# A two-layer graph network: layer 1's weighted rows in buffers of their own, layer 0's gathers by spans

## The chip, the cores and the metric

The kernel runs on one core of one Trainium2 chip. The metric is the device time of one execution in microseconds (us). The core has five engines that run side by side, each through its own list of instructions: TensorE (PE, matrix products), VectorE (DVE, elementwise work), ScalarE (ACT, functions such as exp), GpSimd (POOL, which here mainly issues indirect transfers, the gathers) and SyncE (SP, which issues the other transfers). They wait for each other through semaphores: an instruction that others depend on counts a semaphore up when it is done, and the waiting engine stands still until the count is reached.

## The reference

Everything is float32. x has N = 6250 nodes with C = 256 features; there are E = 100000 edges (src, dst, weight), sorted by dst. Cut to what matters:

```python
# layer 0
xn = layernorm(x)
agg = segment_sum(edge_weight[:, None] * xn[src], dst, N)     # edge loop of layer 0
x = x + relu(agg @ W + b) + linear_attention(xn)
x = x + ffn_top1_of_32(layernorm(x))
# layer 1
xn = layernorm(x)
h = (xn @ W1).reshape(N, 4, 64)                               # 4 heads
e = leaky_relu(h_l[src] + h_r[dst])                           # per edge and head
m = segment_max(e, src, N)
ex = exp(e - m[src])
att = ex / (segment_sum(ex, src, N)[src] + 1e-16)
out = segment_sum(att[:, :, None] * h[dst], src, N)           # edge loop of layer 1
x = x + out + key_value_mix(xn)
x = x + ffn_top2_of_16(x)
```

In layer 1 the edges are grouped by src, the row that is added to; the gathered row is h[dst]. The division by the sum of ex comes after the sums.

## The kernel before, in words

The nodes are 49 tiles of 128 rows. The edges, sorted on the chip by the row that they are added to, are 782 tiles of 128 edges (one edge per partition). Both edge loops do for a tile of edges: gather 128 rows of a table in memory by an indirect transfer on POOL (`gather`, L293 to 296; in the trace its line is L294), make a one-hot matrix S [128 edges x 128 rows] on VectorE, and multiply S^T by the gathered rows on PE into a PSUM tile `ps`; VectorE adds `ps` to the accumulator in SBUF. A float32 product of one tile is two PE instructions in the profile.

**Layer 0's edge loop** (L782 to 800) goes over 196 spans of four tiles. For each tile it gathers into `xg` (24 buffers of one tile), makes S from position and weight in one VectorE instruction (L791, 16 buffers), and multiplies (L793) into the span's `ps` (3 buffers); then two accumulates (L796). Beside it runs the linear attention, one step every second span, and one step of the sort for layer 1 every third span. A gather into a buffer of `xg` waits until the product that read the buffer 24 tiles ago is done, so each product signals.

**Layer 1's edge loop** (L1107 to 1427) goes over 25 chunks of GT = 32 tiles (24 full ones and one of 14). CR = C + 4 = 260 columns: 256 features and four more, which hold h_r of the row until they are replaced by ex, so that one product adds up both the weighted rows and the sums of ex. Three functions are called per chunk, `fetch` one chunk ahead:

- `fetch` (L1236) gathers the chunk's rows of `h_d`, 8 tiles per buffer, into 4 of 8 buffers `hgs`, and loads `pen`, `fr` and the broadcast positions `lob`. Six of the buffers lie in `xs`, a tile [128, 49, 256] that is otherwise the node array; two lie in `hg2`. Then, per 8 tiles: `hw` (L1269, L1271), a transposed one-hot `ST` (L1278) and 8 small products `pe` (L1281), which spread h_l of the rows to the edges.
- `weigh` (L1285) adds the scores (`z`, L1294), finds the segment maxima by scans and transposes on VectorE, and takes exp on ScalarE twice (L1360): once into a PSUM tile `exi`, once into the last four columns of the gathered rows. `fc` (L1363) corrects the accumulator at a chunk's border.
- `gain` (L1377) takes each of the chunk's four groups of 8 tiles: multiplies the gathered rows in place by exp (L1385), makes S (L1388, 2 buffers), does 8 products into `ps` (L1393, 3 buffers) and two accumulates (L1397). After each group it advances a generator, `keys_values` (L1134), which is layer 1's mix: products L1169, L1194, L1228, `sq` L1172, `sd` L1178 and so on.

A gather into a buffer thus waits for the product on PE that read the tile two chunks before. Tile's scheduler puts the instructions of each engine in order and places the semaphores; PE, VectorE and ScalarE each count one semaphore.

After the loop an If (L1680; a fallback, `general_attention`, that these inputs do not take) and then `expert_pairs`, the second feed-forward. It first loads the node array back from memory into `xs` by seven transfers on SP's queue (L1692, L1693; 0.9 MB each, the last smaller), then the weights `w2` (16 loads of 512 KB), the router's weights (L91), and goes on with `finals` (L1726, L1728), the router (product L1714 and its transposes) and the experts.

Of the kernel before, what the change touches and what calls it, by code (L numbers as in the profile page):

```python
# [8 lines left out]
F32 = mybir.dt.float32  # L9
I32 = mybir.dt.int32  # L10
U32 = mybir.dt.uint32
AF = mybir.ActivationFunctionType
OP = mybir.AluOpType
# [7 lines left out]
P = 128  # L21
N = 6250
C = 256
E = 100000
NT = 49
LAST = N - (NT - 1) * P
CH = 7
# [9 lines left out]
TS = (E + P - 1) // P  # L37
SC = 1024
LB = 13
GT = 32  # L40
# [12 lines left out]
def gps_kernel(ctx, tc, x, src, dst, edge_weight, g0_W, g0_b, m0_WqT, m0_WkvT, m0_WpT, m0_bp,  # L53
# [3 lines left out]
    nc = tc.nc  # L57
    cst = ctx.enter_context(tc.tile_pool(name="cst", bufs=1))


    iota = cst.tile([P, P], F32, name="iota")
# [11 lines left out]
    eps = cst.tile([P, 1], F32, name="eps")  # L73
    nc.vector.memset(eps, LN_EPS)

    xs = cst.tile([P, NT, C], F32, name="xs")
    nc.vector.memset(xs[:, NT - 1, :], 0.0)

    CR = C + 4
# [213 lines left out]
    def gather(o, tab, idx):  # L293
        nc.gpsimd.indirect_dma_start(  # L294
            out=o, out_offset=None, in_=tab,
            in_offset=bass.IndirectOffsetOnAxis(ap=idx, axis=0))
# [284 lines left out]
    xw_d = tc.dram_tile([N, C], F32, name="xw_d")  # L581
# [37 lines left out]
    with tc.tile_pool(name="l0", bufs=1) as lp:  # L619
        lo0 = lp.tile([P, 4 * QA], F32, name="lo0")  # L620
        wt0 = lp.tile([P, 4 * QA], F32, name="wt0")
        idx0 = lp.tile([P, 4 * QA], I32, name="idx0")
# [84 lines left out]
        with tc.tile_pool(name="g0w", bufs=4) as gw, tc.tile_pool(name="e0", bufs=1) as ep, \  # L707
# [74 lines left out]
            for b in range(QA):  # L782
                if b % 8 == 0:
                    off = group_values(own0, b, DVE, (NT - 1) * C)
                ps = gps.tile([P, C], F32, name="ps")
                tiles = range(4 * b, min(4 * b + 4, TS))
                for t in tiles:
                    xg = gw.tile([P, C], F32, name="xg", bufs=24)
                    gather(xg, xw_d, idx0[:, t:t + 1])
                    S = gw.tile([P, P], F32, name="S", bufs=16)  # L790
                    nc.vector.tensor_scalar(S, iota, lo0[:, t:t + 1], wt0[:, t:t + 1],  # L791
                                            op0=OP.is_equal, op1=OP.mult)
                    nc.tensor.matmul(ps, S, xg, start=t == tiles[0], stop=t == tiles[-1])  # L793
                for a, m in ((agg, in0[0]), (agg[:, C:], in0[1])):
                    a = a[:, ds(off[b % 8], C)]
                    nc.vector.scalar_tensor_tensor(a, ps, m[:, b:b + 1], a, op0=OP.mult, op1=OP.add)  # L796
                if b % 2 == 1:
                    next(beside, None)
                if b % 3 == 1:
                    next(order, None)  # L800
# [301 lines left out]
            *slots_f0, layer1_rows, order1)  # L1102


    xsf = xs.rearrange("p t c -> p (t c)")
    HU = 8 * CR
    with tc.tile_pool(name="g1", bufs=1) as gp, tc.tile_pool(name="g1b", bufs=2) as gw:  # L1107
        idx1 = gp.tile([P, 8 * QB], I32, name="idx1")
        lo1 = gp.tile([P, 8 * QB], F32, name="lo1")
        hl = gp.tile([P, NT + 1, 4], F32, name="hl")  # L1110
        hg2 = gp.tile([P, 2 * HU], F32, name="hg2")
        nc.sync.dma_start(idx1, idx_d)
        nc.sync.dma_start(lo1, lo_d)
        nc.sync.dma_start(hl, hl_d.rearrange("(t p) k -> p t k", p=P))
        hlf = hl.rearrange("p t k -> p (t k)")

        hgs = [(xsf[:, i * HU:(i + 1) * HU] if i < 6 else hg2[:, (i - 6) * HU:(i - 5) * HU])
               .rearrange("p (i c) -> p i c", c=CR) for i in range(8)]
        zc = gp.tile([P, 1], F32, name="zc")
        nc.vector.memset(zc, 0.0)  # L1120
        nc.scalar.copy(acc, zc.to_broadcast([P, (NT + 1) * CR]))
        with tc.tile_pool(name="g1bp", bufs=1, space=PSUM) as pps:
# [113 lines left out]
            def fetch(t0, n):  # L1236

                hg = []
                for u in range(0, n, 8):
                    h8 = hgs[(t0 + u) // 8 % 8]  # L1240
                    for i in range(min(8, n - u)):
                        t = t0 + u + i
                        gather(h8[:, i, :], h_d, idx1[:, t:t + 1])
                    hg.append(h8)


                pen = gw.tile([P, 33], F32, name="pen")
                fr = gw.tile([4, 2, GT * B], F32, name="fr")
                if n < GT:
                    nc.vector.memset(pen, LOW)  # L1250
                for b in range(B):
                    nc.sync.dma_start(pen[32 * b:32 * b + n, :], bass.AP(
                        tensor=pen_d.tensor, offset=pen_d.offset + t0 * P + 32 * b,
                        ap=[[P, n], [1, 33]]))
                nc.sync.dma_start(fr[:, :, :n * B], bass.AP(
                    tensor=fr_d.tensor, offset=fr_d.offset + t0 * B,
                    ap=[[0, 4], [TS * B, 2], [1, n * B]]))
                brk = gw.tile([P, 2, 4, 32], F32, name="brk")
                for d in range(2):
                    nc.vector.tensor_copy(brk[:, d], pen[:, None, d:d + 32].to_broadcast([P, 4, 32]))  # L1260
                    nc.vector.memset(brk[:, d, :, 31 * d:31 * d + 1], LOW)
                pe = pes[:, t0 // GT % 2]
                ofs = group_values(own1[1], t0 // 8, DVE, (NT - 1) * 4, (n + 7) // 8)
                for u in range(0, n, 8):
                    m = min(8, n - u)
                    q = (t0 + u) // 8

                    hw = gw.tile([P, 4], F32, name="hw", bufs=4)
                    nc.vector.tensor_scalar(hw, hlf[:, ds(ofs[u // 8], 4)], in1[0][:, q:q + 1], None,  # L1269
                                            op0=OP.mult)  # L1270
                    nc.vector.scalar_tensor_tensor(hw, hlf[:, 4:][:, ds(ofs[u // 8], 4)],  # L1271
                                                   in1[1][:, q:q + 1], hw, op0=OP.mult, op1=OP.add)
                    lob = gw.tile([P, 8 * P], F32, name="lob")
                    nc.sync.dma_start(lob[:, :m * P], bass.AP(
                        tensor=lob_d.tensor, offset=lob_d.offset + (t0 + u) * P,
                        ap=[[0, P], [1, m * P]]))
                    ST = gw.tile([P, 8 * P], F32, name="ST")
                    nc.vector.tensor_scalar(ST[:, :m * P], lob[:, :m * P], pcol, None,  # L1278
                                            op0=OP.is_equal)
                    for i in range(m):  # L1280
                        nc.tensor.matmul(pe[:, :, u + i], ST[:, i * P:(i + 1) * P], hw,  # L1281
                                         start=True, stop=True)
                return hg, pe, pen, fr, brk

            def weigh(t0, n, hg, pe, pen, fr, brk, before_):  # L1285
# [70 lines left out]
                nc.vector.tensor_tensor(z[:, :, :n], z[:, :, :n], mx[:, :, :n], op=OP.subtract)  # L1356
                for u in range(0, n, 8):
                    m = min(8, n - u)
                    for o in (exs[t0 // GT % 2][:, u:u + m, :], hg[u // 8][:, :m, C:]):
                        nc.scalar.activation(o, z[:, :, u:u + m].rearrange("p k t -> p t k"), AF.Exp)  # L1360
                if before_ is not None:
                    fc = gw.tile([P, 4], F32, name="fc")
                    nc.scalar.activation(fc, tr[:, 2, :4], AF.Exp)  # L1363
# [13 lines left out]
            def gain(t0, n, hg):  # L1377

                ex = exs[t0 // GT % 2]
                off = group_values(own1[0], t0 // 8, DVE, (NT - 1) * CR, (n + 7) // 8)  # L1380
                for u in range(0, n, 8):
                    m = min(8, n - u)
                    h8 = hg[u // 8]
                    v = h8[:, :m, :C].rearrange("p i (k d) -> p i k d", k=4)
                    nc.vector.tensor_tensor(v, v, ex[:, u:u + m, :, None].to_broadcast([P, m, 4, 64]),  # L1385
                                            op=OP.mult)
                    S = gw.tile([P, 8, P], F32, name="S")
                    nc.vector.tensor_tensor(  # L1388
                        S[:, :m, :], iop[:, None, :].to_broadcast([P, m, P]),
                        lo1[:, t0 + u:t0 + u + m, None].to_broadcast([P, m, P]), op=OP.is_equal)  # L1390
                    ps = pps.tile([P, CR], F32, name="ps", bufs=3)
                    for i in range(m):
                        nc.tensor.matmul(ps, S[:, i, :], h8[:, i, :], start=i == 0, stop=i == m - 1)  # L1393
                    q = (t0 + u) // 8
                    for a, k in ((acc, in1[0]), (acc[:, CR:], in1[1])):
                        a = a[:, ds(off[u // 8], CR)]
                        nc.vector.scalar_tensor_tensor(a, ps, k[:, q:q + 1], a,  # L1397
                                                       op0=OP.mult, op1=OP.add)
                    beside.step()
# [280 lines left out]
    with tc.If(bads1[0] > 0):  # L1680
        general_attention()


    def expert_pairs(ne, nk, hid, w1_d, b1_d, w2_d, b2_d, rw_d, rb_d, ns, xs_d, ys_d):
        lead, step = 104, 3
# [3 lines left out]
        xn_t = xn_d.rearrange("(t p) c -> p t c", p=P)  # L1689
        with ExitStack() as ctx1:  # L1690
            fp = ctx1.enter_context(tc.tile_pool(name="f1", bufs=1))
            for t0 in range(0, NT, CH):  # L1692
                nc.sync.dma_start(xs[:, t0:t0 + CH, :], xs2_d[:, t0:t0 + CH, :])  # L1693
            wt = fp.tile([P, 2, NT], F32, name="wt")
            pi = fp.tile([P, nk * NT], I32, name="pi")
            oi = [fp.tile([1, ns], I32, name=f"own{n}") for n in (1, wn, nf, C)]
# [162 lines left out]
```

## Time and profile before

| | |
|---|---|
| median of 3 runs | 4324.72 us (4312.03 to 4339.27) |
| the profiled execution | 4330.09 us, its span 4328.3 us |
| PE busy | 2628.5 us (61%) |
| VectorE busy | 2106.9 us (49%) |
| POOL busy | 1827.0 us (42%) |
| ScalarE busy | 488.9 us (11%) |
| layer 0's edge loop, first to last gather | 124 to 1282 us |
| layer 1's edge loop, first to last gather | 1872 to 3409 us; its last instruction about 3460 us |
| stage 130 to 1300 us | PE 767, VectorE 564, ScalarE 75, POOL 749 us busy |
| stage 1870 to 3460 us | PE 869, VectorE 767, ScalarE 104, POOL 746 us busy |

How to read it: an engine's busy time is what it worked, not what it waited; the idle time before an instruction is put down to what ended it, its releaser. "remote" means that the instruction waited for a semaphore and that the trace has no instruction whose end fits the moment at which the count came; "issue" means that it waited for nothing that the profile shows. A line such as `L294 POOL DMA_INDIRECT xg<-xw_d,idx x782 | 754.0, 964 | 527.7 <-issue 161.8` reads: line 294, on POOL, 782 gathers from xw_d into xg, busy 754.0 us in all, 964 ns each; POOL was idle 527.7 us ahead of them, most of it (161.8) ended by nothing visible.

### The profile page before, as it was taken

How to read it: one execution, taken by the hardware profiler on the slowest of the kernel's cores; microseconds unless marked ns; L12 is line 12 of the kernel's file. 1: busy time of each engine (PE TensorE's matmuls, PEld its weight loads, DVE VectorE, ACT ScalarE, POOL GpSimd, SP SyncE). 2: the span in 40 equal slices, each digit the busy share in tenths (PEclk: the TensorE clock that was granted, in tenths of full speed). 3: DMA queues.
4: the chain of work that ended last, by engine and by line, in shares of the span. 5: the costliest groups of instructions: out<-in, count | busy, mean ns of one | idle time of the engine just before them, and what ended most of it. 6: DMA issues, size and time to landing. Idle time of an engine off the chain costs nothing. (4 is left out here: it accounts for less than half of the span.)

```text
span 4328.3 us, 43935 instructions
## 1 busy us (share of the span) xinstructions
PE 2628.5 (61%) x11725; PEld 2151.6 (50%) x11725; DVE 2106.9 (49%) x6129; ACT 488.9 (11%) x1386; POOL 1827.0 (42%) x1864
## 2 busy tenths in 40 slices
PE   5466566776776596736465456447556434999920
PEld 4344344555555354625454455446445433788820
DVE  5345454454446566714454455445444654222247
ACT  3000000000001121300111010100000011222200
POOL 0566666666652202253534544454454226000046
PEclk9778787778775565855666666666566655999965
DMA  6633333333321444743333333334444353555544
GB/s 206 203 113 105 103 106 100 98 94 98 101 84 34 155 141 124 204 126 117 110 101 113 109 108 112 109 107 143 144 128 137 92 176 134 189 187 189 185 146 127
DMA packets 355794, 557.64 MB, mean 129 GB/s; under 512 B 91419, under 2 KB 244664, under 8 KB 355270
## 3 DMA queue, kind: packets, MB, share of 16 engines
q0 software_dynamic: 89760, 245.19, 20.3%
q1 hardware_dynamic: 229342, 272.12, 19.7%
q10 hardware_dynamic: 36424, 37.28, 2.6%
q8 instruction: 104, 1.70, 0.2%
q14 instruction: 164, 1.34, 0.1%
HBM read 438.88 MB, written 115.49 MB: 128 GB/s over the span
## 5 line engine op out<-in xcount | busy, mean ns | idle before, releaser
L294 POOL DMA_INDIRECT xg<-xw_d,idx x782 | 754.0, 964 | 527.7 <-issue 161.8
L294 POOL DMA_INDIRECT xs<-h_d,idx x590 | 562.7, 954 | 756.0 <-PE ps L1393 520.4
L1281 PE MATMUL pe<-hw,ST 128*128 128x4 f32 x1564 | 329.0, 341 | 445.7 <-issue 103.4
L1281 PEld LDWEIGHTS pe<-hw,ST 128*128 128x128 f32 x1564 | 329.6, 318 | 455.7 <-issue 102.2
L294 POOL DMA_INDIRECT yg<-f_ys,pi x147 | 172.9, 1176 | 815.5 <-SPq L1792 484.6
L793 PE MATMUL ps<-xg,S 128*128 128x256 f32 x1564 | 456.4, 438 | 72.0 <-DVE S L791 33.4
L793 PEld LDWEIGHTS ps<-xg,S 128*128 128x128 f32 x1564 | 329.8, 223 | 156.9 <-issue 66.0
L1397 DVE SCALAR_TENSOR_TENSOR acc<-ps,in,acc 128x260 f32 x196 | 94.6, 483 | 575.4 <-remote 481.7
L1393 PE MATMUL ps<-xs,S 128*128 128x260 f32 x1180 | 311.5, 431 | 50.9 <-issue 41.8
L796 DVE SCALAR_TENSOR_TENSOR acc<-ps,in,acc 128x256 f32 x392 | 187.3, 478 | 280.8 <-remote 140.5
L1393 PEld LDWEIGHTS ps<-xs,S 128*128 128x128 f32 x1180 | 255.2, 219 | 100.6 <-issue 42.7
L791 DVE TENSOR_SCALAR S<-iota,lo,wt 128x128 f32<-128x128 f32 x782 | 251.2, 352 | 101.7 <-PE ps L793 50.1
L392 POOL DMA_INDIRECT f_xs<-xn,d_pi x147 | 153.1, 1041 | 280.8 <-ACT xT L127 109.9
L294 POOL DMA_INDIRECT hg<-h_d,idx x192 | 183.8, 957 | 97.3 <-remote 49.7
L1781 PE MATMUL y<-w,h 128*128 x856 | 215.4, 392 | 12.6 <-ACT h L1774 9.6
L1769 PEld LDWEIGHTS hT<-xTt,w 128*128 128x128 f32 x1712 | 212.3, 195 | 6.1 <-ACT xTt L127 0.5
L1769 PE MATMUL hT<-xTt,w 128*128 128x128 f32 x1712 | 213.1, 278 | 0.2 <-ACT xTt L127 0.2
L1777 DVE TENSOR_SCALAR h<-hT,b1T 128x128 f32<-128x128 f32 x214 | 74.8, 350 | 254.6 <-ACT h L1774 253.7
L1781 PEld LDWEIGHTS y<-w,h 128*128 128x128 f32 x856 | 149.1, 189 | 48.3 <-ACT h L1774 23.5
L1385 DVE TENSOR_TENSOR xs<-xs,exi 128x2048 f32<-128x2048 f32 x74 | 168.0, 2270 | 6.7 <-ACT exi L1360 6.5
L743 PE MATMUL ctx<-v,k 128*128 128x129 f32 (+1 forms) x196 | 45.1, 368 | 171.1 <-ACT v L741 110.9
L125 PE MATMUL tr<-ident,xt 128*128 128x128 f32 x350 | 86.5, 338 | 80.7 <-DMA xt<-f_xs 80.1
(346 smaller groups left out, 4280.7 us busy)
## 6 DMA issues: line engine op xcount, KB each, us to landing
w<-in_L_ffn_w SPq DMA_DIRECT2D x123, 512.0 KB
lob<-lob_d SPq DMA_DIRECT2D x97, 512.0 KB
xT<-xnT SPq DMA_DIRECT2D x196, 128.0 KB
xt<-f_xs SPq DMA_DIRECT2D x107, 128.0 KB
f_ys<-y SPq DMA_DIRECT2D x107, 128.0 KB
xnT<-xT SPq DMA_DIRECT2D x98, 128.0 KB
xg<-xw_d,idx POOLq DMA_INDIRECT x782
xs<-h_d,idx POOLq DMA_INDIRECT x590
```

The source lines that it names most:

```text
L125: nc.tensor.transpose(p[:, c, :], t[:, c * P:(c + 1) * P], ident)
L294: nc.gpsimd.indirect_dma_start(out=o, out_offset=None, in_=tab, in_offset=bass.IndirectOffsetOnAxis(ap=idx, axis=0))
L392: st = nc.gpsimd.indirect_dma_start(out=xs_d, in_=xn[:r, i, :], in_offset=None, out_offset=bass.IndirectOffsetOnAxis(ap=pi[:r, t, k:k + 1] ...
L791: nc.vector.tensor_scalar(S, iota, lo0[:, t:t + 1], wt0[:, t:t + 1], op0=OP.is_equal, op1=OP.mult)
L793: nc.tensor.matmul(ps, S, xg, start=t == tiles[0], stop=t == tiles[-1])
L796: nc.vector.scalar_tensor_tensor(a, ps, m[:, b:b + 1], a, op0=OP.mult, op1=OP.add)
L1281: nc.tensor.matmul(pe[:, :, u + i], ST[:, i * P:(i + 1) * P], hw, start=True, stop=True)
L1385: nc.vector.tensor_tensor(v, v, ex[:, u:u + m, :, None].to_broadcast([P, m, 4, 64]), op=OP.mult)
L1393: nc.tensor.matmul(ps, S[:, i, :], h8[:, i, :], start=i == 0, stop=i == m - 1)
L1397: nc.vector.scalar_tensor_tensor(a, ps, k[:, q:q + 1], a, op0=OP.mult, op1=OP.add)
L1769: nc.tensor.matmul(hT[:, f, :], w1[:, c, f * P:(f + 1) * P], xT[:, c, :], start=c == 0, stop=c == 1)
L1781: nc.tensor.matmul(yp, h[:, f, :], w2e[:, f * C:(f + 1) * C], start=f == 0, stop=f == nf - 1)
```

## The change

There are three parts.

1. The gathers of layer 1 go into buffers `h8` of their own (8 buffers of 8 tiles). The multiply by exp no longer works in place but writes to `w8` (2 buffers), and the products read `w8`. The second set of exps goes; a copy on ScalarE puts ex into the last columns of `w8` in its place.
2. `xs` now belongs to a pool of its own, which is closed ahead of layer 1's loop and opened again after the If. The seven loads into it stand there.
3. In layer 0 a span of four tiles shares one buffer of `xg` (6 buffers) and of S (4 buffers). The gathers and one-hots of a span are issued from the last tile to the first, and its four products follow together.

The buffer counts make the look-ahead of the gathers 64 tiles in layer 1, as before, and 6 spans of 4 tiles in layer 0, where there were 24 tiles.

```diff
-    xs = cst.tile([P, NT, C], F32, name="xs")
+    def stream():
+        pool = ExitStack()
+        return pool, pool.enter_context(tc.tile_pool(name="xp", bufs=1)).tile(
+            [P, NT, C], F32, name="xs")
+    xpool, xs = stream()
...
-                tiles = range(4 * b, min(4 * b + 4, TS))
-                for t in tiles:
-                    xg = gw.tile([P, C], F32, name="xg", bufs=24)
-                    gather(xg, xw_d, idx0[:, t:t + 1])
-                    S = gw.tile([P, P], F32, name="S", bufs=16)
-                    nc.vector.tensor_scalar(S, iota, lo0[:, t:t + 1], wt0[:, t:t + 1],
+                n = min(4, TS - 4 * b)
+                xg = gw.tile([P, 4, C], F32, name="xg", bufs=6)
+                S = gw.tile([P, 4, P], F32, name="S")
+                for i in reversed(range(n)):
+                    t = 4 * b + i
+                    gather(xg[:, i, :], xw_d, idx0[:, t:t + 1])
+                    nc.vector.tensor_scalar(S[:, i, :], iota, lo0[:, t:t + 1], wt0[:, t:t + 1],
                                             op0=OP.is_equal, op1=OP.mult)
-                    nc.tensor.matmul(ps, S, xg, start=t == tiles[0], stop=t == tiles[-1])
+                for i in range(n):
+                    nc.tensor.matmul(ps, S[:, i, :], xg[:, i, :], start=i == 0, stop=i == n - 1)
...
+    xpool.close()
...
-                    h8 = hgs[(t0 + u) // 8 % 8]
+                    h8 = gw.tile([P, 8, CR], F32, name="h8", bufs=8)
...
-                    for o in (exs[t0 // GT % 2][:, u:u + m, :], hg[u // 8][:, :m, C:]):
-                        nc.scalar.activation(o, z[:, :, u:u + m].rearrange("p k t -> p t k"), AF.Exp)
+                    nc.scalar.activation(exs[t0 // GT % 2][:, u:u + m, :],
+                                         z[:, :, u:u + m].rearrange("p k t -> p t k"), AF.Exp)
...
-                    h8 = hg[u // 8]
-                    v = h8[:, :m, :C].rearrange("p i (k d) -> p i k d", k=4)
-                    nc.vector.tensor_tensor(v, v, ex[:, u:u + m, :, None].to_broadcast([P, m, 4, 64]),
-                                            op=OP.mult)
+                    w8 = gw.tile([P, 8, CR], F32, name="w8", bufs=2)
+                    nc.vector.tensor_tensor(
+                        w8[:, :m, :C].rearrange("p i (k d) -> p i k d", k=4),
+                        hg[u // 8][:, :m, :C].rearrange("p i (k d) -> p i k d", k=4),
+                        ex[:, u:u + m, :, None].to_broadcast([P, m, 4, 64]), op=OP.mult)
+                    nc.scalar.copy(w8[:, :m, C:], ex[:, u:u + m, :])
...
-                        nc.tensor.matmul(ps, S[:, i, :], h8[:, i, :], start=i == 0, stop=i == m - 1)
+                        nc.tensor.matmul(ps, S[:, i, :], w8[:, i, :], start=i == 0, stop=i == m - 1)
...
+    xpool, xs = stream()
+    ctx.enter_context(xpool)
+    for t0 in range(0, NT, CH):
+        nc.sync.dma_start(xs[:, t0:t0 + CH, :], xs2_d[:, t0:t0 + CH, :])
...
-            for t0 in range(0, NT, CH):
-                nc.sync.dma_start(xs[:, t0:t0 + CH, :], xs2_d[:, t0:t0 + CH, :])
```

More of the change, by code (lines that the diff above doesn't have):

```diff
@@ L1102, in gps_kernel @@
             *slots_f0, layer1_rows, order1)
-    xsf = xs.rearrange("p t c -> p (t c)")
-    HU = 8 * CR
+    xpool.close()
     with tc.tile_pool(name="g1", bufs=1) as gp, tc.tile_pool(name="g1b", bufs=2) as gw:
@@ L1110, in gps_kernel @@
         hl = gp.tile([P, NT + 1, 4], F32, name="hl")
-        hg2 = gp.tile([P, 2 * HU], F32, name="hg2")
         nc.sync.dma_start(idx1, idx_d)
@@ L1115, in gps_kernel @@
         hlf = hl.rearrange("p t k -> p (t k)")
-        hgs = [(xsf[:, i * HU:(i + 1) * HU] if i < 6 else hg2[:, (i - 6) * HU:(i - 5) * HU])
-               .rearrange("p (i c) -> p i c", c=CR) for i in range(8)]
         zc = gp.tile([P, 1], F32, name="zc")
```

## The prediction

> **What bounds the kernel now.** I read the page's busy shares first: TensorE (PE) 61%, VectorE (DVE) 49%, GpSimd (POOL) 42%. No engine is full, so some wait decides, and the groups tell which.
>
> ```profile
> L294 POOL DMA_INDIRECT xg<-xw_d,idx x782 | 754.0, 964 | 527.7 <-issue 161.8
> L294 POOL DMA_INDIRECT xs<-h_d,idx x590 | 562.7, 954 | 756.0 <-PE ps L1393 520.4
> L1397 DVE SCALAR_TENSOR_TENSOR acc<-ps,in,acc 128x260 f32 x196 | 94.6, 483 | 575.4 <-remote 481.7
> L1393 PE MATMUL ps<-xs,S 128*128 128x260 f32 x1180 | 311.5, 431 | 50.9 <-issue 41.8
> ```
>
> In layer 1's loop POOL waits 520 us for PE's products and VectorE's accumulate 482 us for something "remote". The tile's view gives first and last gather: layer 0 from 124 to 1282 us, layer 1 from 1872 to 3409 us. The timeline of VectorE in one chunk shows the stall (start, length, engine, line; in brackets the idle time before and its releaser); of the accumulates it has the first of each of the four groups:
>
> ```profile
> 2305.62 2.28 DVE L1385 TENSOR_TENSOR xs<-xs,exi 128x2048 f32<-128x2048 f32 x1
> ...
> 2316.56 0.49 DVE L1397 SCALAR_TENSOR_TENSOR acc<-ps,in,acc 128x260 f32 x1 [2.00 <-PE ps L1393]
> ...
> 2321.44 0.49 DVE L1397 SCALAR_TENSOR_TENSOR acc<-ps,in,acc 128x260 f32 x1 [0.67 <-PE ps L1393]
> ...
> 2341.80 0.49 DVE L1397 SCALAR_TENSOR_TENSOR acc<-ps,in,acc 128x260 f32 x1 [17.98 <-remote]
> ...
> 2351.11 0.49 DVE L1397 SCALAR_TENSOR_TENSOR acc<-ps,in,acc 128x260 f32 x1 [6.12 <-remote]
> ...
> 2356.81 0.21 DVE L1294 TENSOR_TENSOR z<-xs,pe 128x32 f32<-128x32 f32 x1 [5.21 <-remote]
> ...
> 2377.24 2.27 DVE L1385 TENSOR_TENSOR xs<-xs,exi 128x2048 f32<-128x2048 f32 x1
> ```
>
> And PE and POOL in the same stretch:
>
> ```profile
> 2310.10 9.93 PE L1393 MATMUL ps<-xs,S 128*128 128x260 f32 x32
> 2319.87 7.18 PE L1393 MATMUL ps<-hg,S 128*128 128x260 f32 x32
> 2343.82 3.57 PE L1281 MATMUL pe<-hw,ST 128*128 128x4 f32 x16 [16.78 <-DVE hw L1269]
> ```
> ```profile
> 2311.59 0.94 POOL L294 DMA_INDIRECT xs<-h_d,idx  x1 [8.90 <-PE ps L1393]
> 2312.83 0.95 POOL L294 DMA_INDIRECT xs<-h_d,idx  x1 [0.30 <-issue]
> ...
> 2353.82 0.95 POOL L294 DMA_INDIRECT hg<-h_d,idx  x1 [0.30 <-issue]
> ```
>
> PE is through with all 32 products at 2327.05 (2319.87 + 7.18), yet the last accumulate starts at 2351.11: the products were done and their signal was not there. That is 24 us of "remote". The reader sees why beside it: the gathers run without a gap from 2311.59, one per 1.25 us (0.95 + 0.30). In the first 9 us of such a run the products' signals come at once (the first group's ends at 2316.52, its accumulate starts at 2316.56), then some 2 to 4 us pass between one signal and the next. VectorE's own signals are not late. In layer 1 the third and fourth groups of a chunk are 10 to 27 us late throughout; in layer 0 the wait of L796 on "remote" is 140 us.
>
> From this chunk's first multiply (L1385) to the next are 71.6 us; over the loop the mean is 60.1 (2006.2 to 3447.8, 24 chunks). Of it PE is busy some 33 us, VectorE some 30, and 32 gathers at 1.25 are 40.
>
> **The change, part by part.** The profiled execution is 4330.1 us (span 4328.3), 5.4 above the median of 4324.7. I sum against it and take the 5 off.
>
> *Layer 1, products.* Now each of the 32 tiles' products of a chunk signals, since each gather into its rows waits for it. After: 4 signals, one per 8 tiles, and gathers wait for the multiply on VectorE alone. Worked by hand from the start t=0 of a chunk's first multiply, with the durations above: the multiply ends at 2.3 and releases 8 gathers, so the run of 32 starts there (before, at 6.0) and lasts 40 us at best. Group 1's products end at about 11 as now, signal at age 9 or less, on time. The third multiply now needs one of two w8 buffers, that is group 1's products; before, only its one-hot (L1388) did. It moves from 6.7 to some 11.5, group 3's products from 17.9 to 20 or so, group 4's from 21.4 to 25. Each added microsecond counts up to there: some +3 us. Then the signals: four instead of 32, at ages 9 to 23, by 2 to 4 us each as in the runs of now: the last accumulate starts at about 28, against 45.5 in the chunk shown. After it come 20 us (2356.81 to 2377.24: scores, scans, exps, the one-hots ST) as before: period 48. If the last signal takes 16 us, as one did in a free run (next paragraph), it starts at 36 and the period is 56. I take 52, the middle: neither row is nearer, the first has the same matmuls, the second the same gathers. That is 8.1 us off 60.1, over 23 chunks 186 us. The bounds: below, POOL alone; 668 of the 782 starts follow the last by under 1.3 us, so 782 x 1.25 = 978 against 1537 is 559 off, less 50 for the first chunk's two fetches and its weighing (they're in both): -510. Above: +127 (rival D).
>
> The row that speaks against me is at the start of this same loop. There the gathers wait for nothing and PE signals once per 8 tiles, which is what the change makes of the rest (VectorE, then PE):
>
> ```profile
> 1889.65 0.23 DVE L1269 TENSOR_SCALAR hw<-hl,in 128x4 f32 x1 [4.66 <-remote]
> 1906.48 0.23 DVE L1269 TENSOR_SCALAR hw<-hl,in 128x4 f32 x1 [15.89 <-remote]
> 1950.58 0.45 DVE L1269 TENSOR_SCALAR hw<-hl,in 128x4 f32 x1 [42.71 <-remote]
> ```
> ```profile
> 1883.42 6.99 PE L1281 MATMUL pe<-hw,ST 128*128 128x4 f32 x32 [1.13 <-DVE ST L1278]
> 1907.77 3.57 PE L1281 MATMUL pe<-hw,ST 128*128 128x4 f32 x16 [17.36 <-issue]
> ```
>
> Gathers ran from 1871.82 to about 1951. The matmuls that these wait for ended at 1887.0, 1890.4 and 1911.3: late by 2.6, 16 and 39 us, at ages 15, 19 and 39. So fewer signals do not suffice; what counts is how long gathers run unbroken, and the change takes away the pauses that PE's own waits put between them.
>
> *The exps.* Four exps into hg's columns go (0.256 us each), four copies into w8 come, which wait for group u-2's products. ScalarE is 104 us busy of 1590 in this loop; a copy by the nearest row (exp of 128x32) is 0.26 and lies beside the multiply (2.28) and one-hot (1.22) that the products wait for anyway. Zero. Behind a waiting copy on ScalarE stand sq, sd (up to 1.28 for a table) and the next chunk's exps; these come some 30 us later. If the cover went, 4 x 0.26 x 25 = 26 us.
>
> *The buffers.* h8 in a pool of its own with 8 buffers is the same depth as hgs. The first gathers wait 61.8 us for the table h_d anyway, so the new place costs nothing; at most the load of hl (6.4 us wait) comes later: 0 to +7.
>
> *Layer 0.* 782 product signals become 196, the look-ahead sinks from 24 single rows to 6 spans of which one is in use (20 to 24 tiles), and the order within a span is turned so that one wait covers four. Starts now: median 1.25 us apart, 110 gaps over 1.6 us whose excess is 172 us; that is all there is to gain (1158 - 978 = 180). What VectorE waits for remote signals is 140 us, most of it beside gathers. I take 70: the row of POOL's waits for PE here (123 us in 149 waits) with somewhat over half coming back. Bounds: -180, and +60, if the products' signals come late in a smoother run as at 1889 to 1950 and gathers wait on six spans: four of its delays of 16 us. A group now starts when its fourth row has landed: 3 x 1.25 us later, once per span but hidden by 20 tiles of look-ahead (25 us).
>
> *Loads of xs2.* Six of the seven (0.9 MB each) went out on SP's queue at 3412 to 3460, beside the loop's end; now all wait until xs has its place, behind the loop and its If, ahead of 16 loads of w2 (8.4 MB in some 38 us, 220 GB/s). 5.5 MB at that rate are 25 us. Behind them on SP: w2, and the router's weights at 3494, for which TensorE waits until 3505. +25, from 0 (w2's time hides them) to +40.
>
> Sum: 4330 - 186 - 70 + 25 = 4099, less 5: 4095.
>
> [...]
>
> **The rivals.**
>
> B, full release: signals come at once, POOL's gathers bind at 1.25 us. For it: at age under 9 us of a run the signals come at once, as in the chunk shown. Against: 1889 to 1950. 4330 - 510 - 180 + 25 - 5 = 3660.
>
> C, the wait only changes its name: the last group's signal is held to the end of the run of gathers, 2.3 + 40 = 42 us after the multiply; 18 to 20 us of weighing after that give 60 to 62, as now. Then only layer 0 and the loads count: 4330 + 0 - 70 + 25 - 5 = 4280; with layer 0 unmoved 4350. For it: the 39 us at 1950.
>
> D, slower: the second group's signal too is held to the end of its run. The third multiply now waits for PE (w8 has two buffers), and with it the next 16 gathers. Its place is VectorE's queue: behind that multiply stand the accumulates, the next ST and scores. The first 16 gathers end at 22, the next 8, released at 12, at 32; the fourth multiply starts there, its 8 gathers end at 45, and 20 us of weighing give 65.6, 5.5 more than now: 23 x 5.5 = 127. 4330 + 127 + 25 - 5 = 4477 with nothing from layer 0. It decides from the point where a signal at age 9 to 12 takes not the 2 us of now but over 15.
>
> **How the numbers follow.** A, my forecast (partial relief), 0.42: 4095; its own range is 3960 (period 48, layer 0 -130) to 4240 (period 56, layer 0 nothing, loads +40). B 0.16, C 0.18, D 0.24. The range 3680 to 4450 leaves out the half of B below and the half of D above, 0.08 + 0.12 = 0.2. Within 1% (43 us, about what a measurement of this kernel can tell from no change) are 4282 to 4368: most of C. Faster: A 0.42, B 0.16, a quarter of C 0.04 (where signals stay late, layer 0 gives less than its 70 too): 0.62. Same: the rest of C, 0.14. Slower: 0.24.
>
> **What would show it.** In the changed profile: POOL's gathers in layer 1 released by VectorE's L1385 line and no more by PE; the wait of the accumulate on "remote" at about 200 us in place of 482; first multiplies 52 us apart; layer 0's last gather near 1210 instead of 1282; the xs loads behind the loop. I am wrong if the accumulate's "remote" stays at 480 (C), if the multiply itself has waits of over 10 us on "remote" or PE (D), or if the gaps between gathers vanish (B).

## The result

The changed kernel takes 4348.74 us (median of 20 runs, 4333.16 to 4368.09) where the kernel before takes 4333.79 (20 runs, 4312.03 to 4353.32): ratio 1.004, interval 1.0024 to 1.0057. It is slower by 0.4%, where 4095 had been forecast. Two later batches of runs on other chips gave 1.0025 (0.9991 to 1.0059) and 1.0019 (0.9987 to 1.0051).

The groups of the page after (line, engine, operation, output and inputs, count; busy us and mean ns; idle us before them and the releaser of the largest part of it, which need not be most):

```profile
L300 POOL DMA_INDIRECT h<-h_d,idx x782 | 747.5, 956 | 885.7 <-DVE brk L1265 321.8
L1399 PE MATMUL ps<-w,S 128*128 128x260 f32 x1564 | 499.7, 469 | 363.9 <-issue 215.6
L1403 DVE SCALAR_TENSOR_TENSOR acc<-ps,in,acc 128x260 f32 x196 | 94.0, 480 | 675.2 <-remote 550.2
L805 DVE SCALAR_TENSOR_TENSOR acc<-ps,in,acc 128x256 f32 x392 | 187.6, 479 | 412.4 <-remote 267.3
```

The first line agrees with the edit: the largest wait of layer 1's gathers is now for VectorE, and in the profile no wait of theirs is put down to PE any more (before, 520 us). The third shows that it did not help: the accumulate's wait on "remote" rose from 482 to 550 us. The second line's idle time grew too: PE stood 364 us ahead of its products, 216 of it for nothing visible, against 51 before. That is in part a move: ahead of the small products `pe` PE stood 446 us before and 129 after.

One chunk of the changed kernel, VectorE (start, length, engine, line; in brackets idle time and releaser): first multiply, first accumulates of groups 1, 2 and 3, next chunk's first multiply.

```profile
2662.99 2.28 DVE L1388 TENSOR_TENSOR w<-h,exi 128x2048 f32<-128x2048 f32 x1
...
2672.40 0.48 DVE L1403 SCALAR_TENSOR_TENSOR acc<-ps,in,acc 128x260 f32 x1
...
2676.97 0.49 DVE L1403 SCALAR_TENSOR_TENSOR acc<-ps,in,acc 128x260 f32 x1 [0.34 <-PE ps L1399]
...
2710.99 0.49 DVE L1403 SCALAR_TENSOR_TENSOR acc<-ps,in,acc 128x260 f32 x1 [29.78 <-remote]
...
2725.24 2.28 DVE L1388 TENSOR_TENSOR w<-h,exi 128x2048 f32<-128x2048 f32 x1
```

The same stretch on PE, then the first two and the last of the chunk's 32 gathers on POOL:

```profile
2678.90 1.70 PE L1399 MATMUL ps<-w,S 128*128 128x260 f32 x7
2681.24 0.38 PE L1399 MATMUL ps<-w,S 128*128 128x260 f32 x1 [0.65 <-issue]
...
2696.11 0.59 PE L1399 MATMUL ps<-w,S 128*128 128x260 f32 x1 [2.03 <-issue]
...
2709.41 4.59 PE L1399 MATMUL ps<-w,S 128*128 128x260 f32 x9 [0.81 <-issue]
```
```profile
2665.54 0.94 POOL L300 DMA_INDIRECT h<-h_d,idx  x1 [21.97 <-DVE brk L1265]
2666.78 0.95 POOL L300 DMA_INDIRECT h<-h_d,idx  x1 [0.30 <-issue]
...
2704.92 0.94 POOL L300 DMA_INDIRECT h<-h_d,idx  x1 [0.30 <-issue]
```

The gathers run unbroken from 2665.5 to 2705.9. Groups 1 and 2 come through in their first 11 us. From 2681 PE itself mostly goes at one instruction per 0.7 to 2.8 us, and the third group's signal, due at 2689.2 where its products end, comes at 2711.0, 5 us after the last gather. The trace also has the updates of the semaphore that PE counts: after 2676.95 the next one stands at 2710.96. Then PE's instructions come 0.43 us apart at once, the pace at which the next chunk's products start.

The second group is not always let through. Over the 24 full chunks its accumulate starts 5.8 us after its products end on average, 5 us or more in 12 of them and 16 to 21 us in three, as here:

```profile
2953.55 0.49 DVE L1403 SCALAR_TENSOR_TENSOR acc<-ps,in,acc 128x260 f32 x1 [21.66 <-remote]
```

The third group's starts 22.3 us after them on average, the fourth's 9.1. First multiplies are 61.2 us apart (2016.1 to 3485.7, 24 chunks) where they were 60.1.

Stage by stage against the profile before: layer 1's first gather 5 us later (1877.3 against 1871.8); from there to the last product of the loop 1620 us against 1588; from there to the end 852 against 868. Sum +21, the difference of the two spans. The end became shorter, and SP's order fits that, though no run changes it alone. Before, the router's weights went out behind the loads, and the router's first product waited 23.4 us for them:

```profile
3494.36 4.26 SPq L91 DMA_DIRECT2D rw<-in_L_ffn_gate_w  x1
```

Now they are ahead of them, and the router's first product starts at 3515.4, 18 us behind the loop, against 45 before (3505.0):

```profile
3454.89 0.40 SPq L97 DMA_DIRECT2D rw<-in_L_ffn_gate_w  x1
...
3501.99 4.99 SPq L1692 DMA_DIRECT2D xs<-xs_d  x7
```

### The profile page after: what moved, and what is told of

The parts are those of the page before. It is cut to its first block, busy times and chain, and to the rows that moved or that the text cites. A ratio compares the mean times of both kernels' runs of the same rounds, so it can differ in the third digit from the quotient of the medians.

```text
span 4349.7 us, 42258 instructions
## 1 busy us (share of the span) xinstructions
PE 2660.0 (61%) x11725; PEld 2125.8 (49%) x11725; DVE 2092.9 (48%) x6129; ACT 487.2 (11%) x1382; POOL 1828.6 (42%) x1864
## 3 DMA queue, kind: packets, MB, share of 16 engines
q14 instruction: 152, 1.25, 0.1%
## 5 line engine op out<-in xcount | busy, mean ns | idle before, releaser
L300 POOL DMA_INDIRECT h<-h_d,idx x782 | 747.5, 956 | 885.7 <-DVE brk L1265 321.8
L1399 PE MATMUL ps<-w,S 128*128 128x260 f32 x1564 | 499.7, 469 | 363.9 <-issue 215.6
L1399 PEld LDWEIGHTS ps<-w,S 128*128 128x128 f32 x1564 | 361.6, 236 | 485.9 <-issue 266.9
L1285 PE MATMUL pe<-hw,ST 128*128 128x4 f32 x1564 | 286.6, 317 | 129.3 <-DVE ST L1282 76.8
L1285 PEld LDWEIGHTS pe<-hw,ST 128*128 128x128 f32 x1564 | 287.9, 284 | 137.3 <-DVE ST L1282 84.9
L1388 DVE TENSOR_TENSOR w<-h,exi 128x2048 f32<-128x2048 f32 x98 | 222.7, 2273 | 9.4 <-ACT exi L1363 8.7
L749 PEld LDWEIGHTS ctx<-v,k 128*128 128x128 f32 (+1 forms) x196 | 35.3, 247 | 197.2 <-ACT v L747 114.5
```

The lines of the kernel that those rows point to most:

```text
L300: nc.gpsimd.indirect_dma_start(out=o, out_offset=None, in_=tab, in_offset=bass.IndirectOffsetOnAxis(ap=idx, axis=0))
L1388: nc.vector.tensor_tensor(w8[:, :m, :C].rearrange("p i (k d) -> p i k d", k=4), hg[u // 8][:, :m, :C].rearrange("p i (k d) -> p i k d", k= ...
L1399: nc.tensor.matmul(ps, S[:, i, :], w8[:, i, :], start=i == 0, stop=i == m - 1)
```

## The experiments

Theory: signals of PE, few or many, are held as long as gathers follow each other without a break. First rival: each signal costs a few us (the prediction's step), so their number counts. Second: GpSimd's work of any kind holds them. Third: the bytes moved hold them.

The runs come in five batches (a "call" in the expectations); the kernels of one batch share a chip, and times are compared within a batch. This matters here: the kernel before took 4331, 4319 and 4341 us on the chips of three batches and 3625 and 3621 on those of two others. I call the first kind "holding", the second "free"; the traces below say why. Each batch ran on another chip, so a difference between chips and one between batches can't be told apart. TensorE's clock is not the difference: in one kernel that ran on both kinds (`spaced`, below) a product of layer 0 takes 437 ns on the free chip and 438 on the holding one, and the granted clock among the experts is 0.88 in both (3050 to 3650 and 3265 to 3865 us).

**The two parts alone** (holding chip; before 4330.7). `l1_only` takes back layer 0's edit, `l0_only` all but it.

> Layer 1's part and the loads of xs as changed, layer 0's loop as before. The profile of the changed kernel has layer 0's last gather 12 us later than before (1294 against 1282) and layer 1's multiplies 62.9 us apart against 61.6. If these two rows are the parts, this run lies about 12 us below the changed kernel, near 4337. If layer 0's part is innocent and the gap is a matter of the run: about 4349.

> Layer 0's part alone, the rest as before. By the row of the last gather (+12 us) 4346; if a span's single signal helps as the prediction had it, 4265; if it does nothing, 4334.

Measured: l1_only 4354.5, ratio 1.0053 (1.0026 to 1.008); l0_only 4320.9, 0.999 (0.9953 to 1.0026). The loss is layer 1's part; layer 0's shows no effect beyond the noise. Reading its last gather's 12 us as a loss was a miss: l1_only, with the old layer 0, has its last gather at 1295.5.

**Movable breaks** (same batch). After each eighth gather:

```diff
+ for _ in range(4): nc.gpsimd.memset(rest_, 0.0)    # [128, 440]
```

> The changed kernel with four fills of a small tile on GpSimd after each eighth gather of layer 1, estimated at 2 to 4 us together. Theory 1, PE's signals (one or many) are held as long as gathers follow each other without a break: the breaks let them through, the accumulate's wait on remote falls from 550 us to under 250, the multiplies come 50 to 56 us apart, the time is about 4150 to 4250. Theory 2, the signals are held by GpSimd being at work, whatever it does, or the breaks are too short: the remote wait stays, and 97 breaks of 2 to 4 us lengthen the runs, 4350 to 4650.

Measured: 4317.2, ratio 0.9967 (0.994 to 0.9994); remote wait 442 us. Inconclusive: the fills depend on nothing, and the scheduler put most of them where GpSimd was idle anyhow. Where one stretch of 2.8 us fell between gathers (2722.1 to 2724.9), a signal held for 11 us came through at 2726.6.

**Plain transfers in place of gathers** (same batch). Other rows are read, so the sums are of other data:

```diff
- gather(h8[:, i, :], h_d, idx1[:, t:t + 1])
+ r = t * 131 % 6122
+ nc.gpsimd.dma_start(h8[:, i, :], h_d[r:r + P, :])
```

> The changed kernel with layer 1's gathers replaced by plain transfers of 128 consecutive rows, the same bytes, started from GpSimd's queue at the same places (other rows, so the sums are of other data). Theory 1a, it is the making of one descriptor per row on GpSimd that holds PE: no signal is late any more, the accumulate's remote wait goes under 50 us, the multiplies come 34 to 45 us apart, the time is 3650 to 3950. Theory 1b, it is the traffic of 0.13 MB per 1.25 us into SBUF: the remote wait stays at some 500 us, 4300 or more.

Measured: 3642.8 (one run), just under the range expected for no holding. Groups of that profile:

```profile
L1248 POOL DMA_DIRECT2D h<-h_d x782 | 420.8, 546 | 533.8 <-DVE brk L1266 250.9 <-DVE w L1389 67.0 <-DVE xy L1337 65.5
L1404 DVE SCALAR_TENSOR_TENSOR acc<-ps,in,acc 128x260 f32 x196 | 94.1, 480 | 66.4 <-PE ps L1400 65.8
```

The accumulate has no wait on "remote" left, with the same bytes started from the same queue at a faster rate; multiplies come 35.7 us apart. The third rival falls. With three fills ahead of each transfer GpSimd is as busy as with gathers; it ran on a free chip (`direct_busy`, 3745.1) and on a holding one (`direct_busy_b`, 3935.4, one run each):

> The run with plain transfers again (other rows, so other sums), with three fills of 128x260 on GpSimd ahead of each transfer, about 0.9 us: GpSimd is as busy as with gathers, 1.45 us per tile. Theory 1a, the making of descriptors for single rows holds PE: remote waits stay under 50 us; GpSimd then binds at 46 us a chunk, about 3900. Theory 2, any work of GpSimd holds PE: remote waits of 400 us and more, 4300.

> Plain transfers with three fills each (other rows, so other sums). Where signals are not held: 3745 again. Where they are held by the gathers' descriptors alone: 46 to 50 us a chunk and no remote wait, about 3900 (layer 0 still gathers). If held by any work of GpSimd: 4300.

On the holding chip the accumulate waits on nothing but PE, and GpSimd binds at 47.5 us a chunk:

```profile
L1407 DVE SCALAR_TENSOR_TENSOR acc<-ps,in,acc 128x260 f32 x196 | 95.5, 487 | 105.7 <-PE ps L1403 104.8
```

The second rival falls: it is the gathers that hold PE. What in a gather does it, GpSimd's own work on it (956 ns a gather in the profile after, 546 a plain transfer) or the reads of scattered rows, is not separated: the plain transfers differ in both. That this work makes a descriptor for each row, as theory 1a has it, was my assumption; no run shows it.

**Breaks that cannot move.** A fill of the gather's own target has to stay ahead of it. `spaced` fills each tile's place, `spaced64` 64 columns of it, `pinned8` the whole buffer ahead of its 8 gathers:

```diff
+ nc.gpsimd.memset(h8[:, i, :], 0.0)      # spaced; [:64] of it in spaced64
  gather(h8[:, i, :], h_d, idx1[:, t:t + 1])
```
```diff
  h8 = gw.tile([P, 8, CR], F32, name="h8", bufs=8)
+ nc.gpsimd.memset(h8, 0.0)               # pinned8; half8: h8[:, :4, :]
```

First on a free chip (before 3625.4):

> The changed kernel with a fill of the tile's 128x260 place on GpSimd ahead of each gather of layer 1, by the fills of the earlier run (0.46 us for 440 columns) some 0.3 us each: gathers start about 1.6 us apart, and 32 take 51 us. Theory 1, what holds PE builds up while gathers start 1.25 us apart: with a pause behind each the signals come at once, the remote wait goes under 150 us, the multiplies come 51 to 55 us apart, 4080 to 4180. Theory 1b, each gather holds PE for its own time whatever the spacing: the wait lasts to the end of a run that is now 51 us long, the multiplies come 70 us apart, 4500.

> The same with 64 columns filled, an estimated 0.1 us: gathers 1.4 us apart, 32 take 45 us. Theory 1 with a threshold below 1.4 us: as good or better, 4000 to 4150. With a threshold above it, or theory 1b: the signals stay late, 4350 to 4450.

> The changed kernel with the whole buffer of 8 tiles filled on GpSimd ahead of its 8 gathers, some 2.2 us, so that the break cannot move to the end of the run as the four fills of the earlier run did. Theory 1 with breaks of 2 us long enough: remote wait under 250 us, multiplies 48 to 55 us apart, 4000 to 4180. If signals need over 4 us without gathers: a remote wait of about 450 us as with the movable fills, and 4300 to 4400.

Measured: spaced 3755.4, ratio 1.0371 (1.033 to 1.0411); spaced64 3642.9, 1.0037 (1.0012 to 1.0062); pinned8 3736.0, 1.0308 (1.0264 to 1.0351). None of these traces has a remote wait of the accumulate in layer 1. Nothing is held here, and the fills are only GpSimd's time; the times forecast for a holding chip were not put to the test. So I ran them again beside the changed kernel itself, and met a holding chip (before 4319.4):

> The changed kernel unaltered, beside the kernel before on the chip of this call, since the kernel before took 4331 us on the chip of the first experiments and 3625 on that of the second. If PE's signals are held here (before near 4330): ratio 1.004 again, accumulate's remote wait 520 to 560 us. If they are not held here (before near 3625, remote waits near zero): the change takes away only what is left of PE waits on GpSimd and adds PE's wait for w8; by the fills' runs there, which lose 0.4% with 0.18 us of fill per gather, it is 0 to 1.5% faster, 3570 to 3625.

> The whole buffer filled on GpSimd ahead of its 8 gathers (1.85 us, as measured). Where signals are not held: 3736 again, GpSimd binds at 49 us a chunk. Where they are held, theory 1: the breaks let them through, remote wait under 250 us, 4000 to 4180; if a break must be longer: 4300 to 4400.

> A fill of 128x260 (0.34 us) ahead of each gather, starts about 1.6 us apart. Where signals are not held: 3755 again. Where they are held, theory 1: they come at once with pauses, 4080 to 4180; theory 1b, each gather holds PE whatever the spacing: 4400 to 4500.

Measured: after_again 4325.7, ratio 1.0025 (0.9991 to 1.0059); pinned8_b 3982.3, 0.9222 (0.914 to 0.9304); spaced_b 3969.5, 0.9192 (0.9111 to 0.9274). The same loop with more work on GpSimd is 8% faster, and faster than the 4000 to 4180 and 4080 to 4180 expected. The waits of the accumulate, after_again and then pinned8_b (us in total, times, longest):

```profile
DVE acc L1403 <- remote: 526.5, 29, 29.9
```
```profile
DVE acc L1404 <- remote: 102.7, 18, 12.1
```

In layer 1 of spaced_b there is no such line at all. A chunk of it on VectorE (first multiply, first accumulates of groups 1 to 3, first score of the next chunk, next first multiply), and its GpSimd:

```profile
2638.47 2.29 DVE L1389 TENSOR_TENSOR w<-h,exi 128x2048 f32<-128x2048 f32 x1 [1.13 <-ACT exi L1364]
...
2648.38 0.47 DVE L1404 SCALAR_TENSOR_TENSOR acc<-ps,in,acc 128x260 f32 x1
...
2652.51 0.48 DVE L1404 SCALAR_TENSOR_TENSOR acc<-ps,in,acc 128x260 f32 x1
...
2657.05 0.49 DVE L1404 SCALAR_TENSOR_TENSOR acc<-ps,in,acc 128x260 f32 x1 [0.32 <-PE ps L1400]
...
2670.12 0.21 DVE L1299 TENSOR_TENSOR z<-h,pe 128x32 f32<-128x32 f32 x1 [6.68 <-PE pe L1286]
...
2688.47 2.28 DVE L1389 TENSOR_TENSOR w<-h,exi 128x2048 f32<-128x2048 f32 x1
```
```profile
2651.32 0.59 POOL L1247 MEMSET h<- 128x260 f32 x2
2652.06 0.95 POOL L300 DMA_INDIRECT h<-h_d,idx  x1 [0.16 <-POOL h L1247]
2653.32 0.95 POOL L300 DMA_INDIRECT h<-h_d,idx  x1 [0.30 <-issue]
2654.26 0.59 POOL L1247 MEMSET h<- 128x260 f32 x2
```

The third group's accumulate starts 18.6 us after the first multiply, where it started 48 us after it in the changed kernel. Fills and gathers go in pairs, 2.94 us for two, so 1.47 us a gather instead of 1.25. Chunks are 48.3 us apart, as in the same kernel on the free chip, so nothing is held any more; what binds is the gathers: the scores wait 279 us for rows.

**Is it the signals' number after all, how much spacing, and layer 0** (holding chip; before 4340.5). `before_spaced` puts spaced's fill into the kernel before; `both64` adds 64-column fills ahead of layer 0's gathers to spaced64; `after_third` is the changed kernel.

> The kernel before, with the fill of 128x260 ahead of each gather of layer 1 (a signal for each of the 32 products of a chunk, fills and gathers waiting for PE). On a chip that holds signals: if spacing is all that counts, as fast as the changed kernel with the same fills, 3970, multiplies 49 to 50 us apart; if the 28 fewer signals and the earlier release bring something once nothing is held, it stands 50 to 150 us above it, 4020 to 4120. If many signals are held even with spacing: 4300.

> The changed kernel with fills of 64 columns (0.18 us), starts 1.43 us apart, on a chip that holds signals: if what piles up goes away at this spacing too, GpSimd binds at 46 us a chunk, 3880 to 3950, below the 3970 with the longer fill. If the spacing is too small, remote waits come back and the time is 4050 to 4300. On a chip that does not hold them: 3643 again.

> The same with fills of 64 columns ahead of layer 0's gathers too. Layer 0 has 782 gathers in 1170 us; at 1.43 us they take 1118. If the holding is what keeps layer 0 over 1118, its last gather comes at 1245 or so in place of 1294 to 1301, and the run is 30 to 60 us below the one with layer 1's fills alone; if not, it is the same or slower.

> The changed kernel unaltered on the chip of this call: ratio 1.002 to 1.004 if the kernel before takes some 4320 here. If it takes some 3625: what the change is worth where no signal is held, by my account 0 to 1.5% faster, 3570 to 3625.

Measured: before_spaced 4066.5, ratio 0.9369 (0.9308 to 0.9431); spaced64_b 4319.4, 0.9955 (0.991 to 0.9999); both64 4339.6, 1.0009 (0.9969 to 1.005); after_third 4344.4, 1.0019 (0.9987 to 1.0051).

before_spaced has all 32 signals a chunk and its gathers wait for PE, and its chunks are 48.25 us apart, as spaced_b's 48.3; its accumulates wait 1.4 us on "remote" in the whole loop. So in steady state the change's own idea brought nothing here: 61.2 against 60.1 us a chunk where signals are held, and no difference where the gathers are spaced and bind themselves. The time lies in the range that had been expected if fewer signals were worth something, but the 97 us by which it lies above spaced_b are elsewhere. All of its first 64 fills run ahead of the first gather (1723 to 1849 us; the gather at 1877.9), so its first 64 gathers go unspaced, 1.25 us apart; VectorE waits 43.2 us for one signal there, and its first multiply comes at 2015 against 1948. The other part is the end, 884 us from the last first-multiply against 857 (the router's weights again). What is left (3 us) is less than the two batches' kernels before differ.

spaced64_b is held, remote wait 446 us, and its time lies above both ranges expected. Its fills go in twos and threes, and 32 gathers take 41.9 us (2637.4 to 2679.3), 1.35 us each. So 1.35 is too dense and 1.47 is not, on these chips. both64 is held in both layers (remote wait of the accumulates 187 us in layer 0, 437 in layer 1).

**Shorter breaks, and layer 0** (free chip; before 3620.8). `half8` fills half the buffer; `pinned8_l0` adds to pinned8 a fill of `xg` ahead of every second span.

> The changed kernel with half of each buffer filled on GpSimd ahead of its 8 gathers: a break of about 1 us in place of 1.85, every 10 us of gathers. On a chip that holds signals (before near 4330): if a break of 1 us lets them through, GpSimd binds at about 45 us a chunk, 3870 to 3940, below the 3982 with the whole fill. If it is too short, remote waits of 250 us and more and 4100 to 4330. On a chip that does not hold them (before near 3625): about 3660, between the 3736 of the whole fill and the 3643 of the small ones.

> The whole-buffer fill of layer 1 (3982 on a chip that holds signals, 3736 on one that does not), and in layer 0 a fill of a span's 4x256 columns, about 0.9 us, ahead of every second span, so a break of 1 us every 8 gathers. Layer 0's gathers take 1170 us where signals are held and 1000 where not. If short breaks free layer 0 as well, its last gather comes at 1210 to 1230 in place of 1294 to 1305, and the run is 60 to 90 us below 3982. If the break is too short, or layer 0 is held by something else, it is 3980 to 4060.

Measured: half8 3651.7, ratio 1.0076 (1.0049 to 1.0103); pinned8_l0 3831.7, 1.0571 (1.0537 to 1.0604). On a free chip breaks cost nearly what they last: from half8 to pinned8 98 breaks grow from 0.985 to 1.85 us, 85 us in all, and the loss against the kernel before grows by 80. Whether a break of 1 us is enough on a holding chip, and whether it frees layer 0, stays open; so does what the unaltered change does on a free chip, and so whether its idea is worth something where nothing is held and no fill slows the gathers.

half8's layer 0 is that of the changed kernel, and shows what it is without holding (in the tile's view: shortest, median and longest of PE's products, first and last start):

```profile
L802 PE MATMUL ps<-xg,S x1564: 377/379/796, 136.0 to 1131.8; 128*128 128x256 f32 x196
```

In the profile after, on a holding chip, the last of them starts at 1310.0.

## Why the prediction was wrong, step by step

- *What bounds it: late signals of PE.* Right. With plain transfers the waits vanish and the kernel takes 3643; on free chips the kernel before takes 3621 to 3625, near the 3660 worked out for the changed kernel at full release.
- *Layer 1, "Then the signals: four instead of 32, at ages 9 to 23, by 2 to 4 us each".* This is the step that failed. In the rows 28 signals came 2 to 4 us apart while gathers ran, and I took that spacing for a price per signal. In the chunk shown the third group's one signal was 21.8 us late, and PE itself was slowed (the group's products took 10.3 us, 2678.9 to 2689.2, against 3.6 in the chunk before the change). The last group's accumulate, forecast 28 to 36 us after the first multiply, starts 52.5 us after it (2715.47). before_spaced shows the reverse: 32 signals a chunk are not late when gathers are spaced. The row that spoke against the forecast (39 us for a single signal at the loop's start) was the one that measured the case; taking the middle between it and the other gave 52 us a chunk, and it is 61.2. The sum of 48 also has no place for the 5.2 us that the scores waited on "remote" ahead of 2356.81, a late signal like the others.
- *Rival C, "the last group's signal is held to the end of the run of gathers".* This comes nearest: the wait lasts to the end of the gathers, though it is the third group's signal that shows it. Its 4350 with layer 0 unmoved meets the time, partly by luck: its loop was unchanged and its loads +25, measured are +32 and -16.
- *Rival D, the second group's signal is held too.* In part. The third multiply moved to 11.2 us after the first on average (6.7 before), as forecast. In the chunk shown group 2's signal, 10 us into the run, was 1.3 us late, but in three chunks 16 to 21, and the fourth multiply, behind that accumulate in VectorE's queue, came 20.4 us after the first on average, up to 37, against 11.7. The chunk grew by 1.1 us for it, not by D's 5.5.
- *Layer 0, -70.* Nothing beyond the noise came (0.999). Its products' signals are held too: 267 us on "remote" in place of 140, with a quarter of the signals. The bound of -180 was sound: the free chip's loop is 178 us shorter (1131.8 against 1310.0).
- *Loads of xs, +25.* It became -16: I had counted what stands behind the loads on SP, but not that the router's weights would move ahead of them.
- *The forecast's own range, 3960 to 4240.* It doesn't follow from the terms named: period 48 (-278), layer 0 -130 and loads +25 give 3942; period 56 (-94), nothing from layer 0 and loads +40 give 4271.

## What to carry to other kernels

When a signal is late, ask for how long and until what, before counting signals: a delay that lasts to the end of another engine's run is not a price per signal. A row in which the changed condition already holds, even at a loop's edge, outweighs an average over the old condition. And measure on more than one chip where a wait has no visible releaser: breaks in the gathers gave 8% on chips that held signals and cost 3 to 4% on those that did not.

## What the runs showed of the hardware

Unbroken gathers from GpSimd (1.25 us apart) keep PE's signals back (22.3 us on average for the third group of a chunk), and after some 15 us in the chunk shown slow its issuing, on the chips of three batches of five and of the first profiles. At 1.47 us they do not (no remote wait of layer 1's accumulate in spaced_b); with a break of 1.85 us per 8 they hardly do (103 us in pinned8_b, and 47.65 us a chunk against 47.6 on the free chip). VectorE's signals stayed prompt: between 1930 and 3500 us of the changed kernel no instruction of PE or GpSimd has a wait on "remote".

The trace's own records go with it. On a free chip a gather leaves 16 records of its semaphore (15.98 on average): 12,494 of 782 x 16 = 12,512 are there in layer 1 of half8, and all 12,512 for direct_pool's plain transfers on a holding chip. In the changed kernel there are 2326. The two do not go in step, though: spaced_b has 8368 and before_spaced 6249, and hardly an accumulate waits there. Whether the counts themselves come late or only their records are lost, the trace does not tell. Every run on record carries a span and a granted clock from the profiler, so whether PE is held when nothing is recorded stays open, and so does what sets a holding chip apart from a free one.
